# Two convolution layers in one kernel: edge rows copied in DRAM, a fixed VectorE order on q and k, convolutions of v moved, ranks from fewer comparisons

## The chip, the cores and the metric

The kernel runs on one core of a Trainium2 chip. The metric is the device time of one execution in microseconds, the median of several runs. All data are fp32. The core has five engines: TensorE (PE in the profile, PEld where it loads weights), VectorE (DVE), ScalarE (ACT), GpSimd (POOL) and SyncE (SP). Each takes its own instructions in order and waits on semaphores for the others. Transfers run on 16 DMA engines; SP, ACT and POOL issue them.

## What is computed

Two layers, each "x + layer(GroupNorm(x))", on x of shape 1 x 384 x 192 x 192. Cut to what matters:

```python
# layer 0, on GroupNorm(x): 1x1 convolution to 3*384 channels, 2x2 max pooling, 3x3 depthwise
qkv = einsum('bchw,oc->bohw', x, w_qkv) + b_qkv
qkv = qkv.reshape(b, 3*c, 96, 2, 96, 2).max(axis=(3, 5))
qkv = depthwise3x3(qkv, w_dw) + b_dw
q, k, v = split(qkv, 3)                    # 8 heads of 48 channels, 9216 places each
q, k = q / norm(q), k / norm(k)
attn = einsum('bhcn,bhdn->bhcd', q, k) * temperature        # 48 x 48 a head
out = sum(a_i * (topk_softmax(attn, k_i) @ v) for k_i in (24, 32, 36, 38))
out = gelu(out); out = upsample2x2(out); out = einsum('bchw,oc->bohw', out, w_proj) + b_proj
# layer 1, on GroupNorm(x): 7x7 depthwise convolution, its weights averaged over four rotations
```

`topk_softmax(attn, k)` is a softmax over the k largest of the 48 entries of a row; where two are equal, the one with the lower index counts as larger.

## The kernel before

**Layer 0, q and k.** After a stage of statistics (about 150 us), 24 blocks `b` of four pooled rows pass through TensorE (line L663, tile `pq`, 108 products a block). `pooled` lets VectorE take the maximum of each 2x2 window into a ring of rows (`ring`, L673), one ring for each of the six channel tiles `ct`. `bordered` completes the ring's border rows on ScalarE (L695, L699). `depthwise` applies nine taps to a tile (first L706, then L708 eight times, each reading what the one before wrote), VectorE transposes it (L791), ScalarE copies it (`qkT`, L725) and TensorE multiplies the q and k sides (`grams`, `products`, L741). The convolution runs one block ahead of the taps. What is given to `keep` stays in its program order on its engine; the rest is ordered by a scheduler. `pinned` does this for TensorE's instructions alone and puts steps of `products` between the products of L663.

**Layer 0, v.** The image is cut into six strips of 32 rows, and block b of v holds the rows 2b and 2b + 1 of every strip. The 16 blocks are taken in the order 13, 14, 15, 0, ..., 12, so that the strips' bottom and top rows come first. `convolve` makes one channel tile of a third of a block (12 products, L549, tile `pv`) from `xv`, and VectorE reduces it (L555). `xv` is one buffer for three thirds; `load_v` fills a third with three DMAs on SP's queue (L936), once the convolutions of the iteration before have read it. 27 convolutions, those of the first three blocks in the order, run before the loop (`AHEAD = 3`): six of them at the end of q and k, the other 21 given to the scheduler between the steps of `attention`.

**Attention.** `attention` is a generator, advanced between those convolutions. It scales the 48 x 48 products (`scaled`), brings them into `att` with ten small DMAs (L846), and ranks each entry of a row among the 48, for three tiles `mt` of 128 rows each: five instructions on 48 x 48 = 2304 elements a tile, "greater" (L866), "equal" (L868), times `lower`, the mask of lower indices (L870), added (L872) and reduced (L874). Masks from the ranks give the four softmaxes and their mixture (`mix`, L897), which is laid out by small DMAs (`diag`) and transposed for use as weights.

**The loop over v**, `i` = 3 to 15, convolves the block `i` of the order while the block `j = i - 2` goes through `attend`, `project` (L1039) and `residual`. `load_r` fetches the block's x again (`xr`, L1059, SP's queue). `residual` adds (L1076) into `sx`, an SBUF image of runs of 300 elements, and POOL stores this to `sd` in DRAM (L1117, 600 KB each). The three lowest and three highest rows of the strips it stores a second time, shifted, into `sh` in DRAM, as the halos ("edges") of the neighbouring strip (L1127):

```python
for h, shift in halos:
    for q in range(0, NQ, CP):
        nv = min(CP, NQ - q)
        nc.gpsimd.dma_start(
            sh[h + q : h + q + nv, cs].rearrange("f c n -> c f n"),
            rows_of(a, nv, shift + q // CP),
        )
```

These stores come from the blocks 14, 15, 0 and 1, which the iterations `i` = 3 to 6 finish: 54 DMAs, 27.6 MB.

**Layer 1** is a 7x7 convolution as products with banded weights (L1482), reading `sd` and `sh` by ACT's queue (`main`, `aux`, L1227). Its weights (`wt`, `wh`) were made ready by POOL during layer 0.

Of the kernel before, what the change touches and what calls it, by code (L numbers as in the profile page):

```python
# [13 lines left out]
P = 128  # L14
# [72 lines left out]
def conv_preact_d2(  # L87
# [475 lines left out]
    with ExitStack() as bx:  # L563
# [77 lines left out]

        def pinned(ins):

            if ins.ins.engine != mybir.EngineType.PE:
                return ins
            keep(ins)
            while between and next(between[0], between) is between:
                between.pop(0)
            return ins

        def pooled(b, ct, xb):
            rows = xb.rearrange("p t (r c) -> p t r c", c=HW)
            t = ring[ct]
            r0 = 1 + b % 3 * PR
            for g in range(3):
                begun, there = sums_qk.pop((b, ct, g), (None, False))
                ps = begun
                if not there:
                    ps = pq.tile([P, 512], F32, name=f"pq{b}_{ct}_{g}", tag="pq")
                    if begun is not None:  # L660
                        nc.scalar.copy(ps, begun)
                for kt in range(KT) if begun is None else (TWO,):
                    ins = nc.tensor.matmul(  # L663
                        ps,
                        wq[:, kt, ct * P : (ct + 1) * P],
                        rows[:, kt, :, g * 64 : (g + 1) * 64],
                        start=(kt == 0),
                        stop=(kt == KT - 1),
                        skip_group_check=begun is not None,
                    )  # L670
                    if b > 1:
                        pinned(ins)
                nc.vector.tensor_reduce(  # L673
                    t[:, r0 : r0 + PR, 1 + g * 32 : 1 + (g + 1) * 32],
                    ps.rearrange("p (h a w b) -> p h w a b", h=PR, a=2, b=2),
                    AX.XY,
                    ALU.max,
                )

        def biases():  # L680

# [16 lines left out]
            elif b % 3 == 2:  # L698
                nc.scalar.copy(t[:, 0, row], t[:, 3 * PR, row])  # L699

        def taps(dst, ct, win):
            for tap in range(9):
                src = win(tap // 3, tap % 3)
                w = wd[:, ct, tap : tap + 1]
                if tap == 0:
                    nc.vector.tensor_scalar(dst, src, w, bdb[:, ct : ct + 1], ALU.mult, ALU.add)  # L706
                else:
                    nc.vector.scalar_tensor_tensor(dst, src, w, dst, ALU.mult, ALU.add)  # L708

        def depthwise(b, ct, dst):  # L710
            r0 = b % 3 * PR
            taps(dst, ct, lambda i, j: ring[ct][:, r0 + i : r0 + i + PR, j : j + PS])

        Q = 32

# [39 lines left out]
            skip_group_check=True,  # L755
        )
        copies, sides = iter(()), []
        multiplied = None
        for b in range(NB + 1):
            xb = None  # L760
            if b < NB:
                xb = held.pop(b) if b in held else load_x(b, "xq")
            else:

                qx.close()
                pv = psx.enter_context(tc.tile_pool(name="pv", bufs=2, space=PSUM))
                xb = xpool.tile([P, 2 * UT, KT, RB * HW], F32, name="xv_begun", tag="xb")
                for kt in range(KT):
                    nc.sync.dma_start(xb[:, :, kt], image_rows(kt, order[0], 0, 2 * UT))
            done, sides = sides, []  # L770
            for ct in range(2 * KT + 1):
                if ct == (KT if b < NB else 1) and done:
                    between.append(products(b - 2, done))
                if b < NB and ct < 2 * KT:
                    if b == 0 and ct < 2:

                        if ct == 0:
                            pooled(b, 0, xb)
                            pooled(b, 1, xb)
                            biases()  # L780
                    else:
                        pooled(b, ct, xb)
                    bordered(b, ct)
                if b > 0 and ct > 0:
                    dst = qkp.tile([P, PR, PS], F32, name=f"qk{b}_{ct}", tag="qk")
                    depthwise(b - 1, ct - 1, dst)
                    s, t = divmod(ct - 1, KT)
                    if t == 0:
                        turns = trp.tile([P, KT, PB], F32, name=f"turns{b}_{s}", tag=f"turns{s}")
                    flat = dst.rearrange("p h w -> p (h w)")  # L790
                    nc.vector.transpose(turns[:, t], flat)  # L791
                    squares(b - 1, ct - 1, flat)

                    for _ in copies:
                        pass
                    if t == KT - 1:
                        side = trp.tile([P, PB // P, C], F32, name=f"qkT{b}_{s}", tag=f"qkT{s}")
                        sides.append(side)
                        copies = turned(side, turns)
                        for _ in range(2):  # L800
                            next(copies)
                    if b == NB:
                        for n in ((), (), (0, 1), (), (2, 3), (4,), (5,))[ct]:
                            t0 = n // KT * UT
                            convolve(0, t0, n % KT, xb[:, t0 : t0 + UT], pinned)
                        if ct == 2 * KT:
                            for _ in copies:
                                pass
                            between.append(products(b - 1, sides))
                            for left in between:  # L810
                                for _ in left:
                                    pass
            if b == 2:
                for tiles in vrows:
                    row_borders(tiles)
# [5 lines left out]

    def attention(ap):

        rn = const.tile([P, 2 * KT], F32, name="rn")
        nc.vector.tensor_reduce(rn, ssq, AX.X, ALU.add)  # L825
        nc.gpsimd.tensor_tensor(rn, rn, halfpos, ALU.pow)  # L826
# [16 lines left out]
        for i, (mt, r0, r1, h) in enumerate(PIECES):  # L843
# [6 lines left out]
        yield  # L850


        lower = ap.tile([P, HC, HC], F32, name="lower")
        nc.gpsimd.memset(lower, 1.0)
        nc.gpsimd.affine_select(
            out=lower, in_=lower, compare_op=ALU.is_gt, fill=0.0, base=0,
            pattern=[[1, HC], [-1, HC]], channel_multiplier=0,
        )
        rank = ap.tile([P, KT, HC], F32, name="rank")
        for mt in range(KT):  # L860
            full = [P, HC, HC]
            other = att[:, mt, :].unsqueeze(1).to_broadcast(full)
            mine = att[:, mt, :].unsqueeze(2).to_broadcast(full)
            gt = ap.tile(full, F32, name=f"gt{mt}", tag="gt")
            eq = ap.tile(full, F32, name=f"eq{mt}", tag="eq")
            nc.vector.tensor_tensor(gt, other, mine, ALU.is_gt)  # L866
            yield
            nc.vector.tensor_tensor(eq, other, mine, ALU.is_equal)  # L868
            yield
            nc.vector.tensor_tensor(eq, eq, lower, ALU.mult)  # L870
            yield
            nc.vector.tensor_tensor(gt, gt, eq, ALU.add)  # L872
            yield
            nc.vector.tensor_reduce(rank[:, mt, :], gt, AX.X, ALU.add)  # L874
            yield

        row3 = [P, KT, HC]
        top = ap.tile([P, KT], F32, name="top")
# [90 lines left out]
    AHEAD = 3  # L969
    with tc.tile_pool(name="ap", bufs=1) as ap:  # L970
        chain = attention(ap)
        for i in range(AHEAD):
            for t0 in range(0, NT, UT):
                if i > 0 or t0 == 2 * UT:
                    xb = load_v(i, t0)
                    with tc.issue_after(multiplied):
                        for ct in range(KT):
                            convolve(i, t0, ct, xb, lambda ins: ins)
                for _ in range(3):
                    next(chain, None)  # L980
            if i == AHEAD - 1:
                for ct in range(KT):
                    depthwise_v(1, ct, (0, 1))
        for _ in chain:
            pass

# [75 lines left out]
    def residual(i, ot, y, xr, pin):  # L1062
# [43 lines left out]
                yield  # L1106
        cs = slice(ot * P, (ot + 1) * P)

        def rows_of(a, nv, shift):
            o = LEAD + a * RUN + shift  # L1110
            return bass.AP(
                flat.tensor, flat.offset + o, [flat.ap[0], [RB * RUN, nv], [1, RUN]]
            )

        for a in range(RB):
            r = b * RB + a
            nc.gpsimd.dma_start(sdv[r, cs], rows_of(a, CP, 0))  # L1117

            halos = []
            if r >= TR - HALO:  # L1120
                halos.append(((r - TR + HALO) * NQ, -JP))
            if r < HALO:
                halos.append((BOT - TOP + r * NQ, JP))
            for h, shift in halos:
                for q in range(0, NQ, CP):
                    nv = min(CP, NQ - q)
                    nc.gpsimd.dma_start(  # L1127
                        sh[h + q : h + q + nv, cs].rearrange("f c n -> c f n"),
                        rows_of(a, nv, shift + q // CP),
                    )  # L1130


    spare = [(NBC, ct, dy) for ct in range(KT) for dy in (1, 2)]
# [3 lines left out]
    for i in range(AHEAD, NBC):  # L1137
        j = i - 2
        xb = load_v(i, 0)
        for ct in range(KT):  # L1140
            depthwise_v(j, ct, (2,), keep)
            convolve(i, 0, ct, xb, keep)
        gl = attend(j)
        xb = load_v(i, UT)
        for ct in range(KT):
            depthwise_v(i - 1, ct, (0, 1), keep)
            if ct == 1:
# [4 lines left out]
        convolve(i, UT, 2, xb, keep)  # L1152
        ys = [project(j, ot, gl) for ot in range(KT)]
        xb = load_v(i, 2 * UT)
        sums = [residual(j, ot, ys[ot], load_r(j, ot), dve_keep) for ot in range(KT)]
        for ot in range(2):
            for _ in sums[ot]:
# [420 lines left out]
```

## Time and profile before

| | us |
|---|---|
| median of 3 runs (lowest, highest) | 2763.55 (2759.44, 2763.87) |
| the profiled execution | 2786.69 |
| its span | 2784.9 |
| TensorE busy | 2591.1 (93%) |
| VectorE busy | 2456.2 (88%) |
| ScalarE busy | 1140.1 (41%) |
| GpSimd busy | 746.7 (27%) |
| statistics | 0 to 150 |
| 24 blocks of q and k | 150 to 1316 |
| end of q and k, attention, convolutions ahead | 1316 to 1452 |
| loop over v | 1452 to 2121 |
| end of layer 0 | 2121 to 2240 |
| 7x7 convolution | 2240 to 2785 |

The profiled execution took 23 us more than the median of the runs; the durations all come from it. The DMAs moved 581 MB, 209 GB/s in the mean: SP's queue 283 MB, POOL's 149 MB, ACT's 147 MB. Busy shares are means over stages with different limits, so each stage is read by itself. The mean granted clock of TensorE was 0.985 of full speed.

### The profile page before, as it was taken

Reading aid. Unit: us, or ns where it says so; the run is one execution under the profiler, and the core shown is the slowest. Engines: PE = TensorE matmul, PEld = TensorE weight load, DVE = VectorE, ACT = ScalarE, POOL = GpSimd, SP = SyncE. Lnnn points to the kernel's source line nnn. Section 1 sums busy time; section 2 is a strip of 40 time slices with the busy share of each in tenths; the row PEclk is TensorE's granted clock in tenths of the full one; section 3 lists DMA queues with packets and bytes.
Section 4 is the critical chain, followed back from the end, with each engine's and each line's share of the span. In section 5 each row is a group of like instructions: output and inputs, shape, how many; then the busy total and the mean of one; then the engine's idle time right before and its main releaser. Section 6 shows DMA issues by size and latency. Waiting matters only on the chain. (4 is left out here: it accounts for less than half of the span.)

```text
span 2784.9 us, 25837 instructions
## 1 busy us (share of the span) xinstructions
PE 2591.1 (93%) x8365; PEld 1525.2 (55%) x8365; DVE 2456.2 (88%) x3527; ACT 1140.1 (41%) x2262; POOL 746.7 (27%) x885
## 2 busy tenths in 40 slices
PE   0399999999999999999899969999999899999998
PEld 0144444444444444444556646666666677777776
DVE  7989998989999999999789958999889789888886
ACT  0143423333343333433402312232323577777776
POOL 1024443100000000000111321010101478787876
PEclk9999999999999999999899989999999999999999
DMA  9976766301010110110336997566674899999998
GB/s 381 402 252 217 249 213 228 130 34 68 35 68 35 40 62 35 68 35 0 120 103 238 340 362 231 192 230 219 203 246 151 324 343 366 372 375 372 372 374 264
DMA packets 234039, 581.01 MB, mean 209 GB/s; under 512 B 16640, under 2 KB 165744, under 8 KB 217136
## 3 DMA queue, kind: packets, MB, share of 16 engines
q1 hardware_dynamic: 173408, 283.44, 29.0%
q0 software_dynamic: 37376, 148.85, 15.8%
q10 hardware_dynamic: 23120, 147.07, 14.1%
q8 instruction: 67, 1.10, 0.2%
q14 instruction: 68, 0.56, 0.1%
HBM read 370.93 MB, written 208.21 MB: 208 GB/s over the span
## 5 line engine op out<-in xcount | busy, mean ns | idle before, releaser
L663 PE MATMUL pq<-xq,wq 128*128 128x512 f32 x2268 | 1028.8, 597 | 5.4 <-DVE ring L673 4.7
L708 DVE SCALAR_TENSOR_TENSOR qk<-ring,wd,qk 128x384 f32<-128x384 f32 x1152 | 699.4, 616 | 59.5 <-ACT ring L695 32.1
L663 PEld LDWEIGHTS pq<-xq,wq 128*128 128x128 f32 x2268 | 408.7, 190 | 437.3 <-issue 364.0
L549 PE MATMUL pv<-xv,wq 128*128 128x384 f32 x1656 | 545.7, 490 | 26.0 <-DMA xv<-in_x_dram 21.7
L549 PEld LDWEIGHTS pv<-xv,wq 128*128 128x128 f32 x1656 | 316.7, 192 | 245.8 <-issue 20.4
L1482 PE MATMUL pc<-main,w 128*128 128x288 f32 x1536 | 436.4, 406 | 3.0 <-PE al L1515 1.7
L1502 DVE TENSOR_SCALAR apart<-pc,rb 32x576 f32<-32x576 f32 x384 | 312.1, 813 | 81.2 <-PE pc L1482 55.4
L1482 PEld LDWEIGHTS pc<-main,w 128*128 128x128 f32 x1536 | 290.6, 190 | 87.1 <-issue 2.4
L725 ACT COPY qkT<-turns 32x288 f32<-32x288 f32 x768 | 329.0, 428 | 20.7 <-DVE turns L791 9.3
L1500 ACT ACTIVATE apart<-pc,rb 32x576 f32<-32x576 f32 x384 | 281.1, 732 | 133.5 <-PE pc L1482 128.7
L959 DVE SCALAR_TENSOR_TENSOR vb<-rows,wd,vb 128x576 f32<-128x576 f32 x384 | 313.3, 817 | 11.3
L673 DVE TENSOR_REDUCE ring<-pq 128x128 f32<-128x512 f32 x428 | 292.1, 683 | 3.7 <-PE pq L663 3.6
L1482 PE MATMUL pc<-aux,h 128*128 128x288 f32 x768 | 248.1, 405 | 0.0
L719 ACT ACTIVATE junk<-qk 128x384 f32<-128x384 f32 x144 | 71.1, 494 | 411.8 <-DVE qk L708 411.0
L1441 POOL COPY res<-apart 128x1152 f32<-128x1152 f32 (+1 forms) x96 | 222.0, 2338 | 13.3 <-ACT apart L1500 9.5
L826 POOL TENSOR_TENSOR rn<-rn,halfpos 128x6 f32<-128x6 f32 x1 | 1.4, 1359 | 827.5 <-DVE rn L825 827.5
L1076 DVE TENSOR_TENSOR sx<-xr,y 128x576 f32<-128x576 f32 x180 | 203.8, 1173 | 19.9 <-ACT y L1047 14.8
L555 DVE TENSOR_REDUCE rows<-pv 128x192 f32<-128x768 f32 x144 | 137.7, 957 | 84.7 <-PE pv L549 84.6
L1117 POOL DMA_DIRECT2D sd<-sx x96 | 72.2, 755 | 514.5 <-DVE sx L1076 493.2
L741 PEld LDWEIGHTS grams<-qkT,qkT 128*96 128x96 f32 x576 | 92.8, 165 | 147.3 <-issue 136.1
L1096 ACT ACTIVATE wq<-sx,negmid 128x1152 f32<-128x1152 f32 x96 | 120.6, 1257 | 122.5 <-DVE sx L1076 118.2
L1482 PEld LDWEIGHTS pc<-aux,h 128*128 128x128 f32 x768 | 145.1, 189 | 41.2 <-issue 0.2
(227 smaller groups left out, 2270.6 us busy)
## 6 DMA issues: line engine op xcount, KB each, us to landing
sd<-sx POOLq DMA_DIRECT2D x96, 600.0 KB, 10.1
out_dram<-res SPq DMA_DIRECT2D x192, 288.0 KB, 11.2
main<-sd ACTq DMA_DIRECT2D x46, 1200.0 KB, 6.7
xv<-in_x_dram SPq DMA_DIRECT2D x138, 384.0 KB, 6.6
xr<-in_x_dram SPq DMA_DIRECT2D x45, 1152.0 KB, 11.7
xq<-in_x_dram SPq DMA_DIRECT2D x21, 2304.0 KB, 8.2
w<-wt ACTq DMA_DIRECT2D x46, 1024.0 KB
xs<-in_x_dram SPq DMA_DIRECT2D x24, 1536.0 KB, 15.1
```

Source lines behind the costliest of these rows:

```text
L549: nc.tensor.matmul(ps[:, u, 0 : RB * HW], wq[:, kt, o : o + P], xb[:, u, kt, :], start=(kt == 0), stop=(kt == KT - 1),)
L555: nc.vector.tensor_reduce(rows[ct][:, 1 + t0 : 1 + t0 + UT, 1 : PS + 1], ps[:, :, 0 : RB * HW].rearrange("p u (a w b) -> p u w a b", a=2, ...
L663: ins = nc.tensor.matmul(ps, wq[:, kt, ct * P : (ct + 1) * P], rows[:, kt, :, g * 64 : (g + 1) * 64], start=(kt == 0), stop=(kt == KT - 1) ...
L673: nc.vector.tensor_reduce(t[:, r0 : r0 + PR, 1 + g * 32 : 1 + (g + 1) * 32], ps.rearrange("p (h a w b) -> p h w a b", h=PR, a=2, b=2), AX. ...
L708: nc.vector.scalar_tensor_tensor(dst, src, w, dst, ALU.mult, ALU.add)
L725: nc.scalar.copy(side[f * Q : (f + 1) * Q].rearrange("p c (t n) -> p t c n", n=P)[:, :, :, a * Q : (a + 1) * Q], turns[a * Q : (a + 1) * Q ...
L959: pin(nc.vector.scalar_tensor_tensor(dst, src, w, dst, ALU.mult, ALU.add))
L1076: nc.vector.tensor_tensor(bass.AP(flat.tensor, flat.offset + at(e) + a * RUN, [flat.ap[0], [JP, NT], [1, NJ], [at(f) - at(e), 2]],), xq[:, ...
L1441: keep(copy(res[ps, k], apart[ps, :, k].rearrange("p e n -> p n e")))
L1482: nc.tensor.matmul(ahead[q][:, k, 0 : NT * NJ], lhs, rhs, start=(j == 0), stop=(j == 2), skip_group_check=True,)
L1500: keep(nc.scalar.mul(dst, src, scale))
L1502: keep(nc.vector.tensor_scalar_mul(dst, src, scale))
```

## The change

It has four parts.

1. **Edges.** `residual` stores a row once, to `sd`. The edges are then 18 copies from DRAM (`sd`) to DRAM (`sh`) on SP's queue, called in the loop behind `load_v`, from `i` = 7 on, two or three an iteration. Each takes 4 (12 copies) or 2 (6 copies) shifted slabs of 460.8 KB. In the built program the access patterns are [4][8][14400] and [2][8][14400] elements on both sides, and the scheduler puts the first three copies into `i` = 4, 5 and 6.
2. **VectorE's order on q and k.** `pinned` now keeps the order of VectorE too. Taps come from a generator: two taps of a tile behind each of the three poolings of a block's tile, the last three and the transpose behind the poolings of the next tile. The products are put one tile later (`ct == KT + 1`), and `qkT` of the q side has two buffers.
3. **Convolutions of v.** 18 convolutions (the first two blocks of the order; 6 of them were there) come to the end of q and k: twelve beside the last taps, two behind them, and four behind the last products. The nine others stay with the attention.
4. **Ranks.** For each tile, one "greater or equal" of the first 24 entries of a row with the last 24 (576 elements), reduced along both axes, and one within each half (1152 elements), masked by `lower` (now 24 x 24) and reduced along both axes. What entry a gains over b, b loses to a, so each pair is compared once.

```diff
         def pinned(ins):
-            if ins.ins.engine != mybir.EngineType.PE:
-                return ins
             keep(ins)
-            while between and next(between[0], between) is between:
+            while ins.ins.engine == mybir.EngineType.PE and between and next(between[0], between) is between:
                 between.pop(0)
             return ins
-        def pooled(b, ct, xb):
+        def pooled(b, ct, xb, taps):
...
-                nc.vector.tensor_reduce(
+                ins = nc.vector.tensor_reduce(
...
+                if b > 1:
+                    pinned(ins)
+                some(taps, 2)
...
+        def finish(b, ct, dst, taps, now=False):
+            nonlocal copies, turns
+            some(taps, 9)
...
+            ins = nc.vector.transpose(turns[:, t], flat)
+            if b > 0:
+                pinned(ins)
...
+                    t = xpool.tile([P, 2, UT, KT, RB * HW], F32, name=f"xv_begun{n}", tag="xb")
...
+                if b == NB:
+                    if ct == KT - 1:
+                        between.append(products(b - 2, sides[0:2]))
+                    some(taps, 4)
+                    convolve(*xvb.pop(0), pinned)
+                    some(taps, 5)
+                    convolve(*xvb.pop(0), pinned)
+            if b == NB:
+                finish(*last, True)
+                for _ in range(2):
+                    convolve(*xvb.pop(0), pinned)
+                for _ in products(b - 1, sides[2:4]):
+                    pass
+                for args in xvb:
+                    convolve(*args, pe_keep)
...
-            nc.vector.tensor_tensor(gt, other, mine, ALU.is_gt)
-            nc.vector.tensor_tensor(eq, other, mine, ALU.is_equal)
-            nc.vector.tensor_tensor(eq, eq, lower, ALU.mult)
-            nc.vector.tensor_tensor(gt, gt, eq, ALU.add)
-            nc.vector.tensor_reduce(rank[:, mt, :], gt, AX.X, ALU.add)
+            full = [P, HH, HH]
+            nc.vector.tensor_tensor(
+                sq,
+                att[:, mt, 0:HH].unsqueeze(1).to_broadcast(full),
+                att[:, mt, HH:].unsqueeze(2).to_broadcast(full),
+                ALU.is_ge,
+            )
+            nc.vector.tensor_reduce(seconds[:, mt], sq, AX.X, ALU.add)
+            nc.vector.tensor_reduce(
+                firsts[:, mt], sq.rearrange("p d e -> p e d"), AX.X, ALU.add
+            )
+            full = [P, 2, HH, HH]
+            nc.vector.tensor_tensor(
+                tri, halves.unsqueeze(2).to_broadcast(full),
+                halves.unsqueeze(3).to_broadcast(full), ALU.is_ge,
+            )
+            nc.vector.tensor_tensor(
+                tri, tri, lower.unsqueeze(1).to_broadcast(full), ALU.mult
+            )
+            for t, order in ((before, "p s d e -> p s d e"), (behind, "p s d e -> p s e d")):
+                nc.vector.tensor_reduce(
+                    t[:, mt].rearrange("p (s d) -> p s d", s=2), tri.rearrange(order), AX.X,
+                    ALU.add,
+                )
...
-            nc.gpsimd.dma_start(sdv[r, cs], rows_of(a, CP, 0))
...
+            nc.gpsimd.dma_start(
+                sdv[b * RB + a, cs],
+                bass.AP(
+                    flat.tensor, flat.offset + LEAD + a * RUN,
+                    [flat.ap[0], [RB * RUN, CP], [1, RUN]],
+                ),
+            )
+    edges = [
+        (f + h * NQ + q, r + h, shift + q // CP, min(CP, NQ - q))
+        for f, r, shift in ((0, TR - HALO, -JP), (BOT - TOP, 0, JP))
+        for h in range(HALO)
+        for q in range(0, NQ, CP)
+    ]
+    def copy_edge(now):
+        if not now or not edges:
+            return
+        f, r, shift, nv = edges.pop(0)
+        n = CB * RUN
+        nc.sync.dma_start(
+            sh[f : f + nv].rearrange("f (a c) n -> f a (c n)", c=CB),
+            bass.AP(
+                sd.tensor, sd.offset + r * C * RUN + shift,
+                [[TR * C * RUN, nv], [n, C // CB], [1, n]],
+            ),
+        )
...
         xb = load_v(i, 0)
+        copy_edge(i > AHEAD + 3)
...
         xb = load_v(i, UT)
+        copy_edge(i > AHEAD + 3)
...
         xb = load_v(i, 2 * UT)
+        copy_edge(i > AHEAD + 3 and i % 2)
```

## Prediction

> **What bounds the kernel now.** I read the slices of the page first, then stage by stage: the costliest groups, the windows of the two places where TensorE stops, the groups of attention, the DMA issues. Columns of a group: busy us, mean ns | idle us before it, and what ended most of that.
>
> ```profile
> L663 PE MATMUL pq<-xq,wq 128*128 128x512 f32 x2268 | 1028.8, 597 | 5.4 <-DVE ring L673 4.7
> L708 DVE SCALAR_TENSOR_TENSOR qk<-ring,wd,qk 128x384 f32<-128x384 f32 x1152 | 699.4, 616 | 59.5 <-ACT ring L695 32.1
> L549 PE MATMUL pv<-xv,wq 128*128 128x384 f32 x1656 | 545.7, 490 | 26.0 <-DMA xv<-in_x_dram 21.7
> ```
>
> From 150 to 1316 us 24 blocks of q and k pass. TensorE looks full, but it is paced by VectorE. In the timeline matmuls of L663 follow each other every 0.429 us (median) when nothing holds them: 108 x 0.429 + 24 products x 0.084 = 48.4 us a block. The first poolings of successive blocks are 47.8, 47.7 and 52.2 us apart, over and over: 49.5 in the mean. The long one is the block whose border row ScalarE copies (L695); L708 waits for that 32 times.
>
> From 1452 to 2121 us the loop over v takes 49.4 us an iteration, TensorE at its own pitch, with one hole. The windows give busy us of PE, PEld, DVE, ACT, POOL, then clock, DMA share, GB/s:
>
> ```profile
> 1640.00:1650.00 10.00, 0.00 (x0) 0.00 (x0) 2.98 (x3) 3.47 (x8) 5.38 (x8) 0.61 1.04 373
> 1650.00:1660.00 10.00, 2.99 (x4) 1.00 (x4) 0.00 (x0) 0.00 (x0) 0.00 (x0) 0.50 1.04 365
> 1660.00:1670.00 10.00, 6.39 (x11) 3.39 (x11) 0.58 (x1) 0.00 (x0) 0.00 (x0) 0.52 1.04 362
> ...
> 1750.00:1800.00 50.00, 50.00 (x171) 32.30 (x170) 45.55 (x53) 13.77 (x30) 4.50 (x6) 1.00 0.66 216
> ```
>
> The engines of the DMA are full and TensorE waits for xv. The DMA issues of 1490 to 1680 us say what fills them (KB each, median us to landing):
>
> ```profile
> sh<-sx POOLq DMA_DIRECT2D x36, 600.0 KB, 16.2
> ...
> xv<-in_x_dram SPq DMA_DIRECT2D x30, 384.0 KB, 25.5
> sh<-sx POOLq DMA_DIRECT2D x17, 300.0 KB, 16.2
> ```
>
> Over the whole run xv lands after 6.6 us. The 54 edge stores, 27.6 MB, cost a hole: waits of 15.9, 2.2 and 3.6 us, and 47 matmuls that at pitch end at 1653.9 end at 1680.2. That is **26.2 us**. The last 545 us, the 7x7 convolution, the change leaves alone.
>
> Between the two, 1316.4 to 1452.6, lies attention, 136.2 us, where VectorE has the long items:
>
> ```profile
> L866 DVE TENSOR_TENSOR gt<-att 128x2304 f32<-128x2304 f32 x3 | 7.7, 2553 | 0.0
> ...
> L874 DVE TENSOR_REDUCE rank<-gt 128x48 f32<-128x2304 f32 x3 | 7.6, 2543 | 0.0
> ```
>
> [...]the semaphore records show 16 steps for the DMAs of 16 rows and more, but 9 (one, then eight) for the three with 8 rows, the two of `h<-offs` (one of them at 2209 us) and that of `tmpr`. [...]
>
> **The change, part by part.**
>
> *Order on q and k.* Nothing is added; VectorE's order becomes fixed, with two taps behind each pooling, and the last three taps and the transpose of a tile behind the next tile's pooling. From the timeline's pitches: a tap behind a tap of the same tile 0.654 us, behind something else 0.51 to 0.54, pooling to tap 0.60, transpose to tap 0.68. Summed in the new order, a tile takes 7.67 us, six tiles 46.0; before it was 8.25 and 49.5. So 46.0 falls below TensorE's 48.4, and the ring copy is covered. The last L663 product now lies 1125.4 us after the first; 1103.7 of it is work, so at most 21.7 can go. I take **-20** (range -5 to -25: a fixed order can also not step round a late pooling).
>
> *Convolutions and attention.* 18 convolutions (12 matmuls x 0.322 = 3.87 us each) now lie beside the last taps or behind them, 9 left with the ranks. Beside the last taps they add a VectorE reduce of 0.96 each, twelve of them 11.5 us, to a chain that was bounded by VectorE anyway. Following both chains from the end of q and k: last transpose +53.9 us, copies and products +63.3, four convolutions that stand in TensorE's order ahead of the small transposes +78.8, `att` +91, `mix` +134.5, loop +143 to +145. Before, the same points are `att` +56.8, `mix` +126.4, loop +136.2. The ranks themselves lose 15 x 2.55 = 38.3 us and gain per tile one comparison and two reduces on 576 elements and the same with a mask on 1152. [...]with reduces of as many ns as elements and some 110 more (2304 in 2543, L555's 768 in 957), a tile costs 7.4: 0.76 + 2 x 0.69 + 2 x 1.36 + 2 x 1.26. With 1.5 for the small ones that is 23.7, so -15; but `att` comes 34 us later because 18 convolutions and their reduces stand ahead of it. Net **+9** (range 0 to +18, with a colder clock behind about 21 us without TensorE work). Loop start in all: **-11**.
>
> *Edges.* 54 issues of POOL (0.75 us each, 40 us, off the path: POOL is 27% busy) and 27.6 MB from SBUF go: **-26**. In their place SP issues 18 DRAM-to-DRAM copies, 12 of [4][8][14400] and 6 of [2][8][14400] fp32. In the built order one stands in each of i = 4, 5, 6, and 2, 3, 2, 3, 2, 3 in i = 7 to 12, between the loads of xv. The waits on the sd stores are met long before. The bytes would fit if all 16 engines shared them: an iteration moves 216 GB/s x 49.4 us = 10.7 MB, three copies add 4.6, and 15.3 MB at 373 GB/s take 41 us of the 49.4. But the outermost dimension is 4 or 2. [...]the first copies use 4 engines and the second 2, each moving 4 x 460.8 KB / 4 = 460.8 KB[...]. A packet of 9600 bytes took 361 ns in the trace (26.6 GB/s), so a copy holds them **17.3 us**. No trace before has such a copy[...]. It cannot be far under 17.3 on 4 engines, since no packet of the trace goes faster; over 16 engines it is 4.9. I take 17.3: nothing in the trace says that one engine moves less from DRAM to DRAM.
>
> Engine 0 is busy .64 x 49.4 = 31.6 us an iteration already (28.6 at the saturated 373 GB/s). In i = 4 to 6 one copy makes 46 to 49: hidden. In i = 7 to 12 it needs 6 x (28.6 to 31.6) + 15 x 17.3 = 431 to 449 us where TensorE needs 296. A load of xv can start when the previous iteration has read its part, 49.4 - 11.6 = 37.8 us early, less 6.6 to land: 31 us of head start. What is left, 104 to 122, is waiting: **+113** (range +80 to +150; cold clocks fall inside the wait). Queued behind: xv, xr, and SP itself, which reuses eight semaphores and so stops eight DMAs behind a late one. TensorE waits for xv, VectorE for TensorE[...].
>
> **Sum:** -20 + 9 - 26 + 113 = +76 on the profiled 2786.7: 2863. The profiled execution lies 23 above the median of the runs, so 2840; this case's own range 2790 to 2890.
>
> **Rivals.**
> *Spread (25%).* The copies run on 16 engines, at 5 us each, because the dimension counted is not the one that the program shows. For it: the total of bytes fits the loop. Against it: the 8-row DMAs. Then -20 + 9 - 26 = -37 and a few us of contention: 2727 (2712 to 2750). This is the other side. It decides where a copy holds its slowest engine no longer than about 12.5 us: then 15 x 12.5 + 6 x 30 - 296 - 31 is 40, which eats the gain.
> *Few engines at half rate (26%).* [...]3095 (2990 to 3150[...]). [...]
> *The fixed order stalls (within the ranges).* If VectorE's order gained nothing, each case is 15 to 20 later. Poolings at 47.7 us in two blocks of three speak against it.
> *No net change (3%).* A copy near the 12.5 us point.
>
> **How the numbers follow.** Few engines at full rate 46%, at half rate 26%, spread 25%, even 3%. The forecast is the first: 2840. The range runs from the spread case to the middle of the half-rate one, 2715 to 3090, which leaves out about 15%; the likeliest case alone has 2790 to 2890. A difference of 0.2% (5.5 us) is about what a measurement of this kernel can tell from no change. Slower: 46 + 26 = 72%; faster 25%; same 3%.
>
> **What would show it.** Right: semaphore records of the copies with 5 or 3 steps rather than 16; copies that land 20 us or more after issue; a wait of `pv` for `xv` of over 80 us in i = 7 to 13, at a DMA share well under 1; iterations of 65 to 75 us there. Also: poolings 48.4 us apart in every block, no wait of L708 on the ring copy, no hole at 1640, attention some 9 us longer. Wrong: iterations of 49.4 us throughout and copies that land in under 10 us (spread); iterations over 90 us (half rate); blocks still at 49.5 (order).

## The result and the profile after

The changed kernel takes **2868.03 us** (median of 4 runs, 2864.78 to 2870.78) against 2763.71 (4 runs, 2759.44 to 2765.89): 1.0379 times, 95% interval 1.0361 to 1.0397, so 104 us slower. The forecast was slower, 2840, range 2715 to 3090. The profiled execution took 2870.78 us (span 2869.1), 84.1 more than the profiled one before.

These starts come from the timeline (an iteration is counted from its first `gl`):

| us | before | after | difference |
|---|---|---|---|
| last product of L663 / L662 ends | 1316.4 | 1304.1 | -12.2 |
| `att` (VectorE's instruction) starts, from there | +56.8 | +89.4 | |
| `mix` ends, from there | +126.4 | +140.5 | |
| first `gl` of the loop, from there | +150.4 | +160.4 | +9.9 |
| iterations beyond 49.4, i = 3 to 6 | 26.7 | 0 | -26.7 |
| iterations beyond 49.4, i = 9 to 13 | 0 | 26.1, 12.1, 31.3, 13.2, 31.5 | +114.2 |
| first product of the 7x7 convolution | 2209.3 | 2293.4 | +84.1 |
| end | 2784.9 | 2869.1 | +84.2 |

`gl` is ScalarE's first result of `attend`. The four differences add up to 85.2; the last 1.1 us are made up behind the loop.

The costliest groups on the page of the changed kernel (busy us, mean ns | idle before, what ended most of it):

```profile
L662 PE MATMUL pq<-xq,wq 128*128 128x512 f32 x2268 | 1021.9, 596 | 0.0
L717 DVE SCALAR_TENSOR_TENSOR qk<-ring,wd,qk 128x384 f32<-128x384 f32 x1152 | 696.4, 616 | 25.1
L549 PE MATMUL pv<-xv,wq 128*128 128x384 f32 x1512 | 519.8, 505 | 98.7 <-DVE rows L555 81.5
...
L1150 DVE TENSOR_TENSOR sx<-xr,y 128x576 f32<-128x576 f32 x180 | 203.2, 1170 | 110.4 <-DMA xr<-in_x_dram 98.9
```

On q and k TensorE no longer waits for VectorE, and the taps no longer wait for the ring copy. In the loop there is a new wait, and it goes through two engines. VectorE stands before the residual addition (L1150) because xr has not landed; the reduces of the convolutions (L555) are queued behind it on VectorE; and TensorE, whose `pv` buffers they empty, stops. The waits of 1750 to 2125 us (total, times, longest):

```profile
DVE sx L1150 <- DMA xr<-in_x_dram: 98.9, 5, 27.7
...
PE pv L549 <- DVE rows L555: 73.5, 5, 23.0
...
PE pv L549 <- DMA xv<-in_x_dram: 17.0, 9, 2.9
```

The load of the DMA engines in these waits is the reading that matters. First the windows (PE, PEld, DVE, ACT, POOL, then clock, DMA share, GB/s), then the DMA view of 1760 to 1840 us in 40 slices of 2 us (tenths of all 16 engines, and GB/s):

```profile
1784.00:1804.00 20.00, 9.84 (x33) 5.90 (x31) 0.00 (x0) 1.18 (x4) 0.00 (x0) 0.80 0.32 112
1804.00:1824.00 20.00, 7.15 (x18) 4.21 (x19) 16.35 (x16) 8.10 (x12) 4.48 (x6) 0.60 0.95 336
```

```profile
DMA  7279322222229921111103998999998698221547
GB/s 245 110 243 419 135 115 115 115 115 115 95 57 308 333 101 58 58 58 58 58 30 56 357 396 210 366 412 399 372 331 291 225 414 310 96 91 82 171 157 220
```

From 1770 to 1780 us the DMA engines are two tenths busy, at 115 GB/s, and from 1790 to 1800, while VectorE does nothing at all, one tenth, at 58. This is not a lack of bandwidth: before, the hole had a share of 1.04. These are the shares of four, then two engines of sixteen, with twelve or fourteen idle. The trace does not number the engines (the numbers in the forecast and in the expectations are names for those that the copies hold), but its packets say the same: the copies are 480 packets of 57600 bytes, 2.126 us each in the median (27.1 GB/s), four in flight in the first stretch and two in the second (four and two of them in a slice of 2 us make the 115 and 58 GB/s). The two kinds of copy share engines: one of two slabs is issued at 1807.8 us and one of four at 1812.9, and up to 1862 us never more than four of these packets are in flight. The first copy's 32 run from 1512.8 to 1530.8, four at a time. The semaphore records have 14041 steps, before 14779. Take away 54 x 16 for the edge stores, add 3 x 16 for the loads of `xv_begun` that are now 15 more and the loads of xv that are 12 fewer, and add 12 x 5 + 6 x 3 for the copies, and the difference of 738 is met: five and three steps a copy, one more than the packets in flight (the 8-row DMAs of before have nine).

### The profile page after: what moved, and what is told of

It reads as the page before. It is cut to its first block, busy times and chain, and to the rows that moved or that the text cites. A ratio compares the mean times of both kernels' runs of the same rounds, so it can differ in the third digit from the quotient of the medians.

```text
span 2869.1 us, 25691 instructions
## 1 busy us (share of the span) xinstructions
PE 2604.2 (91%) x8365; PEld 1536.1 (54%) x8365; DVE 2452.2 (85%) x3538; ACT 1143.6 (40%) x2262; POOL 702.0 (24%) x831
## 5 line engine op out<-in xcount | busy, mean ns | idle before, releaser
L662 PE MATMUL pq<-xq,wq 128*128 128x512 f32 x2268 | 1021.9, 596 | 0.0
L662 PEld LDWEIGHTS pq<-xq,wq 128*128 128x128 f32 x2268 | 412.2, 191 | 421.5 <-issue 373.7
L549 PE MATMUL pv<-xv,wq 128*128 128x384 f32 x1512 | 519.8, 505 | 98.7 <-DVE rows L555 81.5
L549 PEld LDWEIGHTS pv<-xv,wq 128*128 128x128 f32 x1512 | 296.9, 198 | 312.5 <-DVE rows L555 85.8
L735 ACT COPY qkT<-turns 32x288 f32<-32x288 f32 x768 | 329.4, 429 | 12.1 <-DVE turns L781 3.2
L1150 DVE TENSOR_TENSOR sx<-xr,y 128x576 f32<-128x576 f32 x180 | 203.2, 1170 | 110.4 <-DMA xr<-in_x_dram 98.9
L555 DVE TENSOR_REDUCE rows<-pv 128x192 f32<-128x768 f32 x144 | 137.5, 955 | 76.0 <-PE pv L549 75.9
L1411 DVE SCALAR_TENSOR_TENSOR w<-eye,sb,w 128x512 f32<-128x512 f32 x96 | 167.4, 1782 | 1.5
```

Source lines behind the costliest of these rows:

```text
L549: nc.tensor.matmul(ps[:, u, 0 : RB * HW], wq[:, kt, o : o + P], xb[:, u, kt, :], start=(kt == 0), stop=(kt == KT - 1),)
L662: ins = nc.tensor.matmul(ps, wq[:, kt, ct * P : (ct + 1) * P], rows[:, kt, :, g * 64 : (g + 1) * 64], start=(kt == 0), stop=(kt == KT - 1) ...
L735: nc.scalar.copy(side[f * Q : (f + 1) * Q].rearrange("p c (t n) -> p t c n", n=P)[:, :, :, a * Q : (a + 1) * Q], turns[a * Q : (a + 1) * Q ...
L1150: nc.vector.tensor_tensor(bass.AP(flat.tensor, flat.offset + at(e) + a * RUN, [flat.ap[0], [JP, NT], [1, NJ], [at(f) - at(e), 2]],), xq[:, ...
L1411: nc.vector.scalar_tensor_tensor(mid, eye.unsqueeze(1).to_broadcast([P, 4, P]), sb[:, c : c + 1], mid, ALU.mult, ALU.add,)
```

## Experiments

### The same copies on more engines: e1_outer16, e2_outer8

Only the order of the dimensions differs; bytes, places and queue are those of the change.

```diff
-            sh[f : f + nv].rearrange("f (a c) n -> f a (c n)", c=CB),
+            sh[f : f + nv].rearrange("f (a c) n -> a f (c n)", a=16),        # e2: a=8
             bass.AP(
                 sd.tensor, sd.offset + r * C * RUN + shift,
-                [[TR * C * RUN, nv], [n, C // CB], [1, n]],
+                [[C // 16 * RUN, 16], [TR * C * RUN, nv], [1, C // 16 * RUN]],      # e2: 8 for 16
             ),
```

> The changed kernel, but each edge copy is written with a dimension of 16 outermost: [16][4 or 2][7200], the same bytes at the same places in SP's queue. Theory A (a copy runs on as many DMA engines as its outermost dimension allows, and with 4 or 2 these engines are overloaded in i = 7 to 12): the copies spread over 16 engines, 4.3 us each, no iteration over 50.5 us, the 114 us of waiting go: 2754 (2740 to 2765). Rival B (the DRAM-to-DRAM bytes themselves, or copies standing in SP's queue, hold up xv and xr): still over 2840.

> As the changed kernel, with the copies written [8][4 or 2][14400]: descriptors of 57600 bytes as in the change, on 8 engines by theory A. An nv = 4 copy then holds 8 engines 8.6 us, an nv = 2 copy 4.3, and engine 0 needs at most 190 + 10 x 8.6 + 5 x 4.3 = 298 us in i = 7 to 12 where TensorE needs 296 and 31 of head start are there: theory A says 49.4 us an iteration and 2754 to 2765. Rival C (what costs is the long descriptor of 57600 bytes, which other queues wait for on an engine): the loss stays, over 2830. Rival B: over 2840.

Measured: **2756.06** and **2755.94**, against 2764.44 for the kernel before beside them (ratios 0.9976, interval 0.9961 to 0.9990, and 0.9967, 0.9956 to 0.9978). Every iteration is 49.4 us in both. The loop in e1, in the same stretch of time (columns as above):

```profile
1764.00:1804.00 40.00, 40.00 (x134) 25.26 (x133) 36.13 (x41) 11.54 (x24) 4.49 (x6) 1.00 0.81 295
```

All 112 us went with the order of the dimensions. Rival B falls: the DRAM-to-DRAM bytes and the place in SP's queue are still there. Rival C falls with e2, which has the same descriptors of 57600 bytes, eight at a time, still 2.126 us each (median). The semaphore records have 14251 steps in e1 and 14125 in e2, which is 16 and 9 for each copy in place of 5 and 3. In e1 the DMA view gives a landing time for the large copies, which it does not for those of the change: 12.4 us after issue (median). The packets of e1, 28800 bytes, take 1.067 us each (27.0 GB/s).

### The same copies on fewer engines: e3_pairs

```diff
+        for v in range(0, nv, 2):
+            nc.sync.dma_start(
+                sh[f + v : f + v + 2].rearrange("f (a c) n -> f a (c n)", c=CB),
+                bass.AP(
+                    sd.tensor, sd.offset + (v * TR + r) * C * RUN + shift,
+                    [[TR * C * RUN, 2], [n, C // CB], [1, n]],
+                ),
+            )
```

> As the changed kernel, with each copy of four slabs issued as two copies of two slabs, one behind the other: 30 copies [2][8][14400]. Theory A: all run on engines 0 and 1, 17.3 us each. In i = 7 to 12 these carry 25 pieces in place of 15, 173 us more: about 3040 (3010 to 3075). Rivals B and C: the same bytes in the same descriptors, so 2868 within 15.

Measured: **3077.16** (one execution), 209 above the change. For 479 us exactly two of the packets of 57600 bytes are in flight, for 0.9 three, though the copies of a pair are issued one behind the other: they share the same two engines. The DMA view of 1830 to 1910 us:

```profile
GB/s 51 68 61 58 58 58 58 58 29 58 58 58 58 58 58 58 29 58 168 384 411 287 58 58 58 58 29 58 58 58 58 58 58 58 29 58 58 82 372 332
```

That is A, 2 us over its range. The expectation left out the doubled pieces of i = 4 to 6. These iterations still take 49.4 us, but what the engines have not done by their end is handed on. Counted over i = 4 to 12, these two engines need 9 x (28.6 to 31.6) + 30 x 17.3, less 9 x 49.4 and 31 of head start: 301 to 328 us of waiting. The iterations show 315. The same sum for the change is 93 to 120, measured 114.

### Below the capacity: e12_one_each

The twelve large copies stay on four engines but come one an iteration (`copy_edge(i > AHEAD)` once in the loop); the six small ones are written as in e1.

> The changed kernel with the twelve copies of four slabs still on 4 engines, but one in each of i = 4 to 15, and the six of two slabs written [16][2][7200] in i = 7 to 12. Theory A: engine 0 then needs 28.6 to 31.6 + 17.3 + 2.2 = 48 to 51 us in an iteration of 49.4, which the head start covers: iterations of 49.4 to 51, 2755 to 2765. Rival: any copy on few engines holds up the xv behind it by up to 17 us, and iterations are 55 and more: over 2800.

Measured: **2754.60** (one execution), and every iteration 49.4. So a copy on four engines is not harmful by itself. The loads are later than in e1 (xr lands 19.0 us after issue and xv 9.9, medians; in e1 13.9 and 7.2), but within their head start. It is the sum of an iteration that counts, and the lateness of one iteration handed to the next.

### Another queue: e11_act_queue

```diff
-        nc.sync.dma_start(
+        nc.scalar.dma_start(
             sh[f : f + nv].rearrange("f (a c) n -> f a (c n)", c=CB),
```

> The changed kernel with its copies, [4 or 2][8][14400], issued on ACT's queue in place of SP's (the scheduler then puts all of them into i = 4 to 10). Theory A1: xv and xr are late because on engines 0 to 3 they stand behind the copies in the same queue; [...]the copies may lag behind and nothing waits for them until the 7x7 convolution: the waits fall to less than half, 2770 to 2810. Theory A2: it is the engines' work alone that counts, whatever the queue; 15 copies must be done in the same iterations, 2850 to 2880, or more if ScalarE itself waits to issue.

Measured: **2933.20** (one execution), worse than the change. A1 falls. The iterations i = 4 to 9 take 66.6, 103.1, 67.4, 80.6, 78.8 and 79.2 us, 179 too much; all 18 copies are in i = 4 to 10 here. Counted as above, the engines' work gives 7 x (28.6 to 31.6) + 18 x 17.3 - 7 x 49.4 - 31 = 135 to 156. That leaves at least 23 us that the engines' work alone, theory A2, does not give. The waits of 1450 to 2300 us show that xv, though on a queue without copies, comes late, and that a second thing is in play:

```profile
PEld pv L549 <- DMA xv<-in_x_dram: 133.8, 16, 36.0
PE pv L549 <- DMA xv<-in_x_dram: 122.1, 15, 35.4
...
ACT wq L1170 <- DMA xv<-in_x_dram: 48.1, 1, 48.1
...
ACT gl L1096 <- DMA sd<-sx: 27.8, 1, 27.8
ACT gl L1096 <- DMA xr<-in_x_dram: 26.8, 1, 26.8
...
PE po L1089 <- ACT gl L1096: 13.6, 1, 13.6
...
PE pr L1113 <- ACT gl L1096: 10.5, 1, 10.5
```

ScalarE itself stands still to issue, as A2 allowed: three of its waits (27.8, 26.8 and 48.1 us) end with the issue of a copy, and during the first two TensorE waits 24.1 us for `gl`. That is the size of what was left over, but no run separates it from the copies' earlier place in the loop. How an engine divides itself between the two queues was not measured either.

### The hole of the kernel before: e4_before_again, e9_old_edges

> The kernel before, unchanged, for a second profile. The first profiled execution took 23 us more than the median of the runs. If that lies in the hole at 1640 us (theory: how far the edge stores delay xv differs from execution to execution), this profile, if it is near 2764, shows a hole of under 8 us and an iteration of under 58 us in place of 76. If it lies elsewhere, the hole is again about 26 us and another stage is shorter by some 20.

Measured: **2755.18** (one execution) with an iteration of 53.9 where the first profile has 76.1. TensorE's waits of 1440 to 1700 us in the first profile and in this one:

```profile
PE pv L549 <- DMA xv<-in_x_dram: 21.7, 3, 15.9
```

```profile
PE pv L549 <- DMA xv<-in_x_dram: 2.3, 2, 1.4
```

22.2 of the 31.5 us between the two profiles are this hole; another 7.4 lie ahead of the end of q and k. The DMA engines are full in both, but move more in this one: over 100 us around the beginning of the hole, 366 against 384 GB/s (means of five windows), and in the window in which the hole begins, 1620 to 1640 us of the first profile and 1630 to 1650 of the second, 344 against 398. That the lower rate makes the hole is likely from this, but no run changed the rate alone.

```profile
1620.00:1640.00 20.00, 18.92 (x68) 12.54 (x66) 18.91 (x23) 5.13 (x13) 5.03 (x7) 1.00 1.03 344
```

```profile
1630.00:1650.00 20.00, 17.70 (x51) 10.02 (x50) 14.05 (x14) 8.25 (x17) 9.49 (x13) 0.91 1.04 398
```

The time of the kernel before also differed between the three comparisons, each on another chip: 2764.44, 2788.38 and 2761.60 (medians). The second is near the first profile's 2786.69; that its runs have the large hole is likely, but none of them was profiled.

e9 is e7 (below) with the edge stores of the kernel before in place of the copies:

> e7_early12 with the edge stores of the kernel before (54 from SBUF on POOL's queue in i = 3 to 6, no copies). Theory: the stores fill the DMA engines in i = 3 to 6, and the hole is back, of a size that differs between executions (4.5 and 26.7 us in two profiles of before): slower than e10_best of the same chip by 4 to 30 us, and spread over more than 10. Rival: without the hole's cause in the other parts (VectorE's order, the time at which the loop starts) it stays small, under 4 us.

Measured: **2744.13** against 2743.08 for e10_best beside it. The rival holds: the iteration is 49.9, the DMAs move 369 to 402 GB/s in the stretch, and there is no hole. So even copies on sixteen engines gained nothing measurable over the old stores here. Whether the DMA rate or the other parts of the change kept the hole away is open, and what the copies would gain where the rate is low was not tried with everything else equal.

### The order on q and k: e5_order_free

```diff
         def pinned(ins):
+            if ins.ins.engine != mybir.EngineType.PE:
+                return ins
             keep(ins)
```

> e1_outer16 with pinned keeping TensorE's order alone, as before; the instructions and where the program names them stay those of the change. Theory: the fixed order is what takes the blocks of q and k from 49.5 to 48.7 us; free, poolings come again at 47.5, 47.7 and 52.4 and q and k end 8 to 15 us later: 2763 to 2771. Rival: the new place of the taps in the program does it by itself, and 2756 stays within 3.

Measured: **2773.54**. The poolings come at 51.6, 47.7 and 47.9 us again, where the fixed order has 48.71 every time, and the q and k stage is 9.7 us longer than in e1 (1136.7 against 1127.0 from its first product; the change and e1, with the same code there, differ by 1.9). The first `gl` is another 5.9 later after it. The theory holds; the total is 2.5 over its range. (e1, with which this and the next three runs are compared, is from the first comparison, on another chip; so the readings are taken from the traces.)

### The ranks: e6_old_ranks

The function `attention` is that of the kernel before as far as the ranks.

> e1_outer16 with the ranks of the kernel before (15 instructions of 2.55 us in place of some 23 us). Theory: VectorE's chain from att to mix sets the end of this phase, so all of it shows: 15 us later, 2771 (2766 to 2776). Rival: TensorE's convolutions set the end, and VectorE has room: 2756 to 2760.

Measured: **2767.91**, 11.9 above e1: inside the range of the theory, but not by the 15 us that it rests on. In the traces 8.8 lie between the end of q and k and the loop. Another 2.8 lie ahead of it, where the two programs are the same, so these are not the ranks'. VectorE's groups of e1 from `att` to `mix` (1390 to 1442 us) say why:

```profile
L935 DVE TENSOR_REDUCE behind<-tri 128x48 f32<-128x1152 f32 x3 | 9.0, 2995 | 0.0
...
L917 DVE TENSOR_REDUCE firsts<-sq 128x24 f32<-128x576 f32 x3 | 4.7, 1569 | 0.0
L925 DVE TENSOR_TENSOR tri<-att 128x1152 f32<-128x1152 f32 x3 | 4.1, 1352 | 0.0
...
L935 DVE TENSOR_REDUCE before<-tri 128x48 f32<-128x1152 f32 x3 | 4.0, 1343 | 0.0
L909 DVE TENSOR_TENSOR sq<-att 128x576 f32<-128x576 f32 x3 | 2.2, 749 | 0.0
L916 DVE TENSOR_REDUCE seconds<-sq 128x24 f32<-128x576 f32 x3 | 2.2, 746 | 0.0
```

The comparisons cost what was said (0.76 and 1.36 us in the forecast, 0.749 and 1.352 here). But a reduce along the other axis, with neighbours 24 elements apart, takes 2.995 us where the one along the rows takes 1.343, and 1.569 against 0.746. With the masking (L930, 1.35) a tile costs 10.1 us, not 7.4; three tiles and 1.5 are 31.8, so by this sum the new ranks save 6.5 of the 38.3 and not 15. The time from `att` to `mix` differs by 7.5 (58.4 in e6, 50.9 in e1).

### The convolutions of v: e7_early12, e8_early6

```diff
-                for n in range(3):                                  # the tiles of xv_begun
+                for n in range(2):                                  # e8: 1, one convolution a tile of taps
...
-                for _ in range(2):
-                    convolve(*xvb.pop(0), pinned)                   # those behind the taps
...
-        i = AHEAD - 1
-        for t0 in range(0, NT, UT):
+        for n in range(4, 9):                                       # e8: range(2, 9)
+            i, t0 = divmod(n * UT, NT)
```

The numbers of steps of `attention` between these convolutions, left out here, were changed to suit.

> e1_outer16 with 12 convolutions of v beside the last taps, and none of the six behind them and behind the last products; these come among the steps of the ranks (15 there). Theory: the six stand in TensorE's order ahead of the small products that scaled and att wait for, about 6 x 3.87 = 23 us, of which the 9.9 that the phase lost are a part: att 20 us earlier, loop start 8 to 14 earlier, 2742 to 2748. Rival: the convolutions only change places with idle time, 2753 to 2760.

> e1_outer16 with 6 convolutions beside the last taps, as many as before, and 21 among the steps of the ranks. Theory: att at about +57 us from the end of q and k as before, but then 21 convolutions of 3.87 us are 81 us of TensorE behind it, so TensorE sets the end: within 5 of e7, 2743 to 2752. Rival: VectorE has the reduces of all 21 in its chain of ranks and mix comes as late as in the change: 2753 to 2760.

Measured: **2742.31** and **2762.00**. From the end of q and k, `att`, `mix` and the first `gl` come at +73.7, +125.9, +146.4 in e7 and at +68.9, +126.0, +164.0 in e8; in e1 at +89.3, +140.2, +160.6, and in the second profile of before at +56.7, +126.2, +150.3. TensorE's timelines (start, length, instruction [idle before]) of e1, e7 and e8 show what each waits for. The parts are cut to the stretch from the last products of `grams` to `aT`, the transposes that end attention:

```profile
1361.79 2.11 PE L751 MATMUL grams<-qkT,qkT 128*96 128x96 f32 x22 [0.90 <-ACT qkT L735]
1363.73 15.67 PE L549 MATMUL pv<-xv_begun,wq 128*128 128x384 f32 x48
1379.34 0.82 PE L877 MATMUL tps<-tmpr,hsel 8*128 8x1 f32 x6
...
1444.46 2.20 PE L984 MATMUL aT<-ident,diag 128*128 128x128 f32 x7 [18.49 <-DMA diag<-mix]
```

```profile
1353.04 0.82 PE L875 MATMUL tps<-tmpr,hsel 8*128 8x1 f32 x6
...
1362.01 3.83 PE L751 MATMUL grams<-qkT,qkT 128*96 128x96 f32 x22 [1.13 <-ACT qkT L735]
...
1413.58 19.62 PE L549 MATMUL pv<-xv,wq 128*128 128x384 f32 x60 [1.49 <-DVE rows L555]
1433.03 0.93 PE L982 MATMUL aT<-ident,diag 128*128 128x128 f32 x7
```

```profile
1407.66 43.02 PE L549 MATMUL pv<-xv,wq 128*128 128x384 f32 x132 [1.08 <-DVE rows L555]
1450.52 0.93 PE L980 MATMUL aT<-ident,diag 128*128 128x128 f32 x7
```

In e1, and so in the change, `tps`, the small transposes that `att` needs, stands behind four convolutions that are fixed ahead of it (15.67 us), and later TensorE has nothing left and waits 18.5 us for `diag`. In e8 the ranks are done as early as in e7, but eleven convolutions stand ahead of `aT`: TensorE sets the end, and "within 5 of e7" was wrong by 15. In e7 the two chains end together. So the loss of this phase, +10 us, lies in the six convolutions ahead of the ranks: without them there the first `gl` comes 14.2 us earlier.

### The best version: e10_best

> e7_early12 once more: order on q and k, the new ranks, 12 convolutions early, edges copied on 16 engines. 2742 (2739 to 2746), and under the kernel before by 10 to 46 us, since the time of before has depended on the chip (2764 and 2788 in the two comparisons) and this one has no hole.

Measured: **2743.08** (2742.10 to 2744.89), the kernel before beside it 2761.60: 0.9930 (0.9905 to 0.9956). The first comparison of the same program, as e7, gave 2742.31 and 0.9840 (0.9818 to 0.9862), with 2788.38 for before. The new time hardly moves between the two comparisons; the kernel before does.

## Why the prediction was right, and where it was off

**Edges: right, and settled.** The step that decided the sign was that copies with 4 and 2 outermost run on as many DMA engines; in the trace of before only the nine steps of the 8-row DMAs spoke for it. The semaphore records of the change, e1 and e2, with 16, 9, 5 and 3 steps a copy, and the packets in flight of e3 bear it out for 16, 8, 4 and 2. The price of 17.3 us a copy measured 8 packets x 2.126 = 17.0; the half rate, which held 26% of the chance and which no trace of before showed, is refuted by it. +113 was forecast, +114.2 measured. The sum of the engines' work, counted from i = 4 on, holds for e3, e12 and the change, and leaves at least 23 us of e11.

**The chain of that wait: half right.** TensorE was to wait over 80 us for xv. It waits 17.0 for xv and 73.5 for VectorE, which waits 98.9 for xr. The xr loads stand in the same queue, later than xv; the prediction named them but did not follow who waits for them on VectorE. SP, whose DMAs use eight semaphores in both traces, waited only 16.1 us for DMAs from 1750 to 2125 us. The place differs too: the iterations are long in i = 9 to 13, not from i = 7 on, since the head start lasted to i = 8.

**Order on q and k: mechanism right, -12.2 instead of -20.** The mis-sized term is TensorE's floor. 108 x 0.429 + 24 x 0.084 gave 48.4 us a block; with no idle time at all a block takes 48.71. Over the stage's 23 further blocks that is about 8 us, the whole difference. Why a block takes the 0.36 us more stays open.

**Convolutions and attention: +9.9 against +9, but by two errors that cancel.** `att` came at +89.4 (said: +91) and `mix` at +140.5 (said: +134.5), since the ranks take 31.8 us by the sum under e6 and not 23.7; the strided reduces are nearly all of that. The first `gl` followed at +160.4, that is 19.9 behind `mix`, where before it was 24.0 and the prediction left this distance about as it was. That the net came out at +9.9 is luck. TensorE's longest wait there was 17.4 us, for `diag`, and the granted clock was 0.50 behind it (1440 to 1450 us).

**The hole: the step that failed.** -26.7 was measured between the two profiles, as said. But the sum then took off another 23 for the distance of the profiled execution from the median of the runs, as though the changed kernel had the same distance. The second profile of before shows otherwise: 22.2 of the 31.5 us between the two profiles are the hole, so most of the distance was the hole itself, and it was counted twice. The changed kernel's profile lies 3 us from its median, not 23. How large the hole is in a median run of before was not measured: the run of 2755 us has 4.5, and at the same share of hole (22.2 of 31.5) one of 2764 would have about 10, an estimate. The result is 2868, 28 above the forecast: 20 from this, 8 from the order on q and k.

## What to carry to other kernels

Look at the outermost dimension of a long DMA. Here the same bytes in the same queue cost 112 us more with 4 and 2 outermost than with 16, or with 8, and the sign of it was a share of one or two tenths with everything waiting. Copies on four engines, one an iteration, cost nothing (2754.60 us, every iteration 49.4): sum the work of the engines that every copy uses. Before costing a stall from one profile, ask whether the typical run has it: a profiled execution 23 us above the median was itself the warning. When work is moved ahead of a chain, count who stands behind it in the engine's order: six convolutions ahead of the ranks cost 14 us that they could have spent beside them.

## What the hardware showed that was not expected

A VectorE reduce along an axis whose neighbours lie 24 fp32 elements apart took 2.2 times one along the row (2.995 against 1.343 us for 1152 elements). Copies from DRAM to DRAM ran at 27.1 GB/s an engine with packets of 57600 bytes, no slower than the packets of 9600 bytes before (361 ns, 26.6 GB/s). Putting the long copies on another queue did not let the loads pass (TensorE waited 122.1 us for xv; 2933 against 2868 us). With full DMA engines, the rate that two executions of the same kernel reached differed by 5% over 100 us (366 and 384 GB/s), and the hole that followed by 22 us.
